# A two-layer graph network on one core: chunks 3 and 0 turned into features in halves, one more place for tiles, and a fixed list of eight steps in the second sweep

## Chip, core and metric

The kernel runs on one core of a Trainium2 chip. The metric is the time of one execution on the device in microseconds. The kernel before took 341.48 us (median of three runs, 340.38 to 344.35).

## What is computed

`x` has 4096 nodes with 64 features each. `adj` is a 4096 x 4096 float32 matrix in which about one entry in 128 is not zero. Two layers follow each other, each with a residual:

```python
h = relu(layernorm(x))                       # layer 0: two hops, x1 and x2
for k in range(2):
    h = tanh(concat([adj @ h, h]) @ W[k])
x = x + h
h = relu(layernorm(x))                       # layer 1: weighted neighbours
support = h @ weight
mask = adj != 0
rank = cumsum(mask, axis=1); deg = rank[:, -1:]
k = minimum(deg, 100); pos = rank - (deg - k)
w = mask * where(pos > 0, 0.5 ** (k - pos), 0)
x = x + w @ support + bias
```

Layer 0 needs the values of `adj` twice, once for each hop, and the second hop of a row needs the first hop of all rows. Layer 1 needs only where `adj` is not zero, and how many such entries follow in the same row: the weight of an entry is a power of two with that number as exponent.

## The kernel before

The 4096 nodes are four chunks of 1024 (CW), each of eight blocks of 128 (CB). A tile is a piece of `adj`, transposed by the host: 128 source nodes of one block by the 1024 destination nodes of one chunk, 512 KB. "Chunk" stands for destinations (I) or sources (J or g), "block" (b) for 128 sources.

**Sweep 1** reads all of `adj`, 1 MB (two blocks) at a time, row of chunks by row of chunks (0, 1, 2, 3). TensorE forms the first hop of each row from the weighted features (`acc_low`, L302), and for sources whose x1 is known already a part of the second hop (`acc`, same line). VectorE and ScalarE turn each tile into a byte code per entry (L267 to L283), which stays in SBUF: `code[g][J]` is 8 KB per partition for a pair of chunks. `settle` (L471) brings the codes of a row into their last form, once the row's counts are known. The tiles pass through a ring of five places of two blocks each, and through code places that are not filled yet.

`hxs[q]` holds for chunk q, per block, 64 columns of x1 (or h) and behind them 64 columns of the weighted features (`at(b)[:, :D]` and `at(b)[:, D:]`). There are four such tiles; `hx0` is reused when sweep 1 is over.

**Sweep 2** (`sweep2`, from L931) finishes layer 0 and does layer 1. Its work for TensorE is of three kinds:

- Hops (`hop`, L302 by `agg_pair`, and L987): 72 blocks of `adj` are read again, in the order `plan`: two or more blocks of chunk 2, eight of chunk 3, the rest of chunk 2, 24 of chunk 1, 24 of chunk 0. A block is two matmuls of 64 columns x 512, which the profile records as four; it needs its tile from HBM (L949, L951).
- The way from a chunk's sum to its layer-1 features (`finish_x2`), a chain across engines: copy the sum (L685 or L688), multiply (`py`, L697), add (L703), tanh (L707), residual (L712), layer norm (L196 to L202, with a power on GpSimd, L202, and the bias on GpSimd, L718), scale and maximum (L205), split into a high and a low part (`feat`, L743, L744). [...]
- Units of layer 1 (`layer1`, L870): 128 units, one for each source chunk J, destination chunk g and tile n. A unit is two matmuls of 128 columns x 512. It needs the features of chunk J and its weights, which are made from the codes by ScalarE in one instruction (an exponential, L810) or by VectorE in two (L802 makes the bits of a power of two, L805 scales it). Weights need a place of 4 KB per partition (`spaces`): ring pairs that are no longer loaded, code pairs whose units are done, the `after` rows, `hx1`, `hx2`; `hx0` holds the bits of VectorE's conversion.

The sums of a destination chunk over several J stay in PSUM where `kept` has the pair (four pairs). Else they are evicted to `parts` and added there (`evict`, L895 to L901). `finish_out` (L918, L925) multiplies by the layer's weight, adds, and writes out.

What sets the order: every engine runs its own instructions in the order in which the program emits them, and the program is written by a planner. `clock` holds the planner's estimate for each engine (a block 0.86, a unit 0.465, a conversion 0.96 on ScalarE and 1.4 on VectorE), `use` advances it, and tiles have an estimated landing. Before, the loop at the end of `sweep2` goes on with hops as long as tiles have landed by the estimate, and with units where they are runnable, but leaves 56 units (`n_late`) for after the last hop. `decode` decides which engine converts the next weights; `run_chain` resumes `finish_x2` when its clock is reached. SP issues all loads in the same order, each after the place it writes has been read.

Of the kernel before, what the change touches and what calls it, by code (L numbers as in the profile page):

```python
# [19 lines left out]
P = 128  # L20
# [24 lines left out]
def gnn_kernel(  # L45
# [50 lines left out]
    hxs = [place([P, CB, 2 * D], F32, f"hx{q}", "hx") for q in range(NCH)]  # L96
    at = lambda b: hxs[b // CB][:, b % CB, :]
# [129 lines left out]
    def weighted(I):  # L227

        v = by_t(flat(pre1[:, chunk(I), :]))
        pt = (one if I % 2 else two)(name="pg")  # L230
        for t in range(TC):
            nc.tensor.matmul(  # L232
                pt[:, t * P : (t + 1) * P].rearrange("p (c e) -> p c e", c=NC),
                v[:, t // 2, t % 2, :], wz[:, :, 0, 0, :],
                start=True, stop=True, skip_group_check=True,
            )
        nc.scalar.copy(
            as_nodes(hxs[I][:, :, D:]), pt.rearrange("p (t c e) -> p t c e", t=TC, c=NC)
        )
# [79 lines left out]
    def features_T(I):  # L319

        pt = (two if I % 2 else one)(name="ph")
        for t in range(TC):
            for c in range(NC):
                nc.tensor.matmul(
                    pt[c * D : (c + 1) * D, t * P : (t + 1) * P],
                    hxs[I][:, c * TC + t, :D], ident, start=True, stop=True, skip_group_check=True,
# [53 lines left out]
    def finish_first(acc, quads):  # L380
# [4 lines left out]
        def x1_half(c):  # L385
# [14 lines left out]
            for h in range(2):  # L400
                nc.scalar.copy(
                    as_nodes(hxs[0][:, :, :D])[:, 2 * h : 2 * h + 2, c], nodes(banks[h])[:, :, 0, c]
                )

        def hop1(b):
            for c in range(NC):
                nc.tensor.matmul(  # L407
                    G[c * D : (c + 1) * D, :], at(b)[:, :D], part_of(quads[c, b // 4], b),
# [33 lines left out]
    def finish_row(I, acc):  # L442
# [9 lines left out]
        take(hxs[I][:, :, :D], banks, 0)  # L452
# [26 lines left out]
    def sweep1():  # L479
        b0 = NB - CB // 2  # L480
        load_x(NCH - 1)
        first = ln_relu(hxs[-1][:, CB // 2 :, :D], pre1[:, b0:, :])
# [53 lines left out]
        for k in range(2 * NQ):  # L536
# [15 lines left out]
            if k == 0:  # L552
                rest = ln_relu(hxs[-1][:, : CB // 2, :D], pre1[:, NB - CB : b0, :])
                for g in (2, 1, 0):
                    lns[g] = ln_relu(hxs[g][:, :, :D], pre1[:, chunk(g), :])
                ends = []
                for n in (CB // 2, 0):
                    v = slice(n, n + CB // 2)
                    ends.append(ln_relu(hxs[2][:, v, :D], pre1[:, 2 * CB :, :][:, v]))
# [6 lines left out]
            for b in (4 * q + n for n in (2, 3, 0, 1)):  # L566
                h = b % 2
                nc.tensor.matmul(  # L568
                    low0[c][h * D : (h + 1) * D, :], at(b)[:, :D], part_of(a, b),
# [28 lines left out]
        for k in range(2 * NQ, len(units)):  # L598
# [16 lines left out]
            for r in (1, 0):  # L615
                g = b - 1 + r
                last = n == HB - 1 and r == 0
                agg_pair(acc[1], at(g)[:, D:], a[:, r], g == NB - 1, last)
                if fused(I, g):
                    agg_pair(  # L620
                        acc[0][:, 0, :], at(g)[:, :D], a[:, r], g == (3 if I == 1 else CB * I - 1), last
# [26 lines left out]
    def finish_last(acc):  # L648
# [10 lines left out]
        take(hxs[I][:, :, :D], banks, 0)  # L659
# [19 lines left out]
    def finish_x2(I, acc):  # L679


        h = chunk(I)
        S = tmp(name="S")
        if clock["ACT"] <= clock["DVE"]:
            nc.scalar.copy(S, acc)  # L685
            t = use("ACT", 0.6, clock["PE"] + 0.2) + 0.1
        else:
            nc.vector.tensor_copy(S, acc)  # L688
            t = use("DVE", 0.7, clock["PE"] + 0.2) + 0.1
        xres = residual(I)  # L690
        state["gap"] = 1.35, 2.2
        yield t

        pt = one(name="py")
        v = by_t(S)
        for t in range(TC):
# [5 lines left out]
        y = tmp([P, CB, D], name="y")  # L702
        nc.vector.tensor_tensor(  # L703
            as_nodes(y), pt.rearrange("p (t c e) -> p t c e", t=TC, c=NC), as_nodes(pre1[:, h, :]),
            op=ALU.add,
        )
        nc.scalar.activation(y, y, AF.Tanh)  # L707
        t = use("DVE", 0.7, use("PE", 1.15, t) + 0.2)
        state["gap"] = 0.6, 2.7
        t = use("ACT", 0.65, t + 0.1)  # L710
        yield t - 0.5
        nc.vector.tensor_add(pre1[:, h, :], xres, y)  # L712
        state["fetch"] = True
        t = use("DVE", 0.7, t + 0.1)
        ln = ln_relu(None, pre1[:, h, :])
        next(ln)
        t = use("DVE", 1.4, t)
        nc.gpsimd.tensor_tensor(  # L718
            pre1[:, h, :], pre1[:, h, :],
            bias_b[:, None, :].to_broadcast([P, CB, D]), op=ALU.add,  # L720
        )
        state["gap"] = 0.0, 1e9
        t = use("ACT", 0.65, t + 0.1) + 0.1
        yield t
        next(ln)
        t = use("POOL", 2.6, use("DVE", 0.9, t) + 0.1) + 0.1
        yield t
        try:
            next(ln)
        except StopIteration as stop:  # L730
            h2 = stop.value
        t = use("DVE", 0.7, t)
        while (
            state["done"] < CB * NCH * (2 - I)
            or I == 2 and any(w is lent[2] for w, _ in made[state["done"] :])
        ):
            yield clock["PE"] + 0.3
        if I == NCH - 1:
            feats[I] = feats[1] = place([P, CB, 2 * D], F32R, "mbuf", "feat")
        elif I == 0:  # L740
            feats[I] = feats[2]
        hi, lo = feats[I][:, :, :D], feats[I][:, :, D:]
        nc.vector.tensor_scalar(hi, h2, SCALE, None, op0=ALU.mult)  # L743
        nc.vector.scalar_tensor_tensor(  # L744
            lo, h2, SCALE, hi.bitcast(F32), op0=ALU.mult, op1=ALU.subtract
        )
        ready[I] = use("DVE", 1.2, t + 0.1) + 0.2


# [29 lines left out]
    order = {3: (0, 1, 2, 3), 2: (3, 0, 1, 2), 1: (2, 3, 0, 1), 0: (0, 1, 2, 3)}  # L779
    kept = {(3, 3), (2, 2), (1, 0), (1, 1)}  # L780
    units = [(J, g, n) for J in range(NCH - 1, -1, -1) for g in order[J] for n in range(CB)]
# [6 lines left out]
    state = {"wide": True, "fetch": True, "done": 0, "lead": 5.0, "dve": False, "dlead": 2.0, "gap": (0.0, 0.0)}  # L788

    def convert(engine=None):  # L790
        i = len(made)
        J, g, n = units[i]
        spaces.sort(key=lambda v: v[1])
        w, t = spaces.pop(0)
        v = (J, g, n % 2)
        if v in settled:
            settle(settled.index(v))
            done[J, g] = use("DVE", 1.25)
        t = max(t, done.get((J, g), 0.0) + 0.1)
        q = code[g][J][:, n, :]  # L800
        if engine == "DVE" or not engine and state["dve"] and max(clock["ACT"], t) + 0.96 > max(clock["DVE"], t) + 1.4:
            nc.vector.tensor_scalar(  # L802
                state["bits"], q, float(ZERO), ONE, op0=ALU.subtract, op1=ALU.mult
            )
            nc.vector.tensor_scalar(  # L805
                w, state["bits"].bitcast(F32), 2.0 ** (127 - LOW), None, op0=ALU.mult
            )
            t = use("DVE", 1.4, t)
        else:
            nc.scalar.activation(w, q, AF.Exp, scale=LN2, bias=BIAS)  # L810
            t = use("ACT", 0.96, t)
        made.append([w, t + 0.1])

    def decode():
        while True:
# [5 lines left out]
            if ahead <= 2 and state["done"] < len(units) and units[state["done"]][0] in ready:  # L821
# [7 lines left out]
            t = min((v[1] for v in spaces), default=1e9)  # L829
            if n == len(units):  # L830
                t = 1e9
            act, dve = (max(clock[e], t) for e in ("ACT", "DVE"))
            late = clock["DVE"] <= clock["PE"] + state["dlead"]
# [4 lines left out]
            elif (  # L838
                state["dve"] and late and dve + 1.4 <= d_end and dve <= clock["PE"] + 3.0
                and dve + 1.4 < act + 0.96 + (0.0 if len(spaces) < 3 else 1.0)  # L840
            ):
                convert("DVE")
# [261 lines left out]
```

## Time and profile before

| | |
|---|---|
| median of the runs shown | 341.48 us (340.38 to 344.35) |
| the profiled execution itself | 343.04 us |
| its span in the profile | 341.3 us |
| granted TensorE clock | 1.00 |
| TensorE busy | 329.6 us, 1578 matmul records |
| VectorE busy | 280.4 us |
| ScalarE busy | 190.5 us |
| read from HBM | 107.15 MB |

By stretches of the span (us from its start; busy time of each engine; what the DMA moved):

| stretch | what it is | length | PE | VectorE | ScalarE | GB/s |
|---|---|---|---|---|---|---|
| 26.6 to 191.9 | sweep 1 after its start | 165.3 | 165.3 | 153.7 | 75.6 | 304 to 421 |
| 194.4 to 207.5 | first hops of sweep 2 | 13.1 | 13.0 | 9.2 | 4.0 | 365 |
| 207.5 to 223.8 | hops up to the first unit | 16.3 | 14.6 | 9.5 | 3.0 | 408 |
| 223.8 to 255.7 | hops of chunk 1, first units | 31.9 | 31.9 | 22.2 | 18.1 | 405 |
| 255.7 to 303.0 | hops of chunk 0, units | 47.3 | 47.3 | 39.6 | 44.9 | 213 |
| 303.0 to 315.4 | units while chunk 0 becomes features | 12.4 | 10.9 | 11.3 | 10.4 | 0 |
| 315.4 to 341.3 | last units and outputs | 25.9 | 22.3 | 14.4 | 16.6 | 41 |

In the profile PE is TensorE's matmul, PEld its weight load, DVE is VectorE, ACT ScalarE, POOL GpSimd and SP the engine that issues the DMAs. "L302" is line 302 of the kernel. A name such as `accl` is a tile of the program. The profile says of an idle stretch which instruction's end released the waiting one. Matmuls are pipelined and their ends are modelled, so that TensorE can look busy while it runs below its pace. One execution is profiled; its instruction durations are used below.

### The profile page before, as it was taken

To read this page: it belongs to the slowest core of one execution; us is meant where nothing else is said; L and a number is where in the kernel's file an instruction comes from. 1 tells how busy PE (TensorE), PEld (TensorE's weight loads), DVE (VectorE), ACT (ScalarE), POOL (GpSimd) and SP (SyncE) were. 2 spreads that over 40 slices of the span, in tenths; PEclk is the share of its full clock that TensorE was granted. 3 is DMA by queue.
4 is the path that set the end of the run, shared out by engine and by line. 5 is a ranking of instruction groups with operands and counts; after the bars stand their busy time and mean duration, and the time that the engine had idled before them with its cause. 6 is when DMAs were issued, how large, how long until landed. Compare 5 with 4: busy or idle time off the path is not lost.

```text
span 341.3 us, 4305 instructions
## 1 busy us (share of the span) xinstructions
PE 329.6 (97%) x1578; PEld 150.1 (44%) x1578; DVE 280.4 (82%) x439; ACT 190.5 (56%) x199; POOL 23.5 (7%) x21
## 2 busy tenths in 40 slices
PE   8699999999999999999999999899999999998995
PEld 2354433433334333343333433143454656466885
DVE  4869999999999999999969683779456799889933
ACT  2493673285444590233480424037468999969990
POOL 2340000000000000000000000312003000003000
PEclk9999999999999999999999999999999999999999
DMA  7999999999999889976999999999996946500012
GB/s 265 420 423 420 424 415 427 418 422 421 421 418 423 371 321 419 356 270 219 381 361 292 324 356 411 409 409 407 407 396 237 344 151 219 198 17 0 2 52 71
DMA packets 22404, 108.47 MB, mean 318 GB/s; under 512 B 2416, under 2 KB 3824, under 8 KB 14320
## 3 DMA queue, kind: packets, MB, share of 16 engines
q1 hardware_dynamic: 22384, 108.21, 81.3%
q8 instruction: 12, 0.20, 0.2%
q14 instruction: 8, 0.07, 0.1%
HBM read 107.15 MB, written 1.05 MB: 317 GB/s over the span
## 4 chain that ended last, share of the span: by engine, by line
PE 82%; DMA 12%; DVE 3%; ACT 1%; SPq 0%; issue 0%
PE acc_low L302 25%; PE acc L302 20%; PE accl L870 16%; PE acc L987 6%; DMA codes<-in_adjA_dram 5%; DMA ring<-in_adjA_dram 5%; PE acc L568 4%; PE pto L918 2%; PE acc L407 2%; DMA wb<-in_weights_dram 2%; PE pt L370 2%; PE py L697 1%; PE acc_low L568 1%; PE po L215 1%; PE pg L232 1%; PE pt L396 1%
## 5 line engine op out<-in xcount | busy, mean ns | idle before, releaser
L810 ACT ACTIVATE weights<-codes 128x1024 fp32r<-128x1024 uint8 x91 | 87.6, 1044 | 7.0 <-PE accl L870 4.4
L302 PE MATMUL acc<-ring,hx 128*64 128x512 f32 x352 | 86.3, 597 | 1.7 <-DMA ring<-in_adjA_dram 1.7
L302 PE MATMUL acc_low<-ring,hx 128*64 128x512 f32 x264 | 65.5, 593 | 0.0
L870 PE MATMUL accl<-weights,feat 128*128 128x512 f32 x254 | 62.9, 399 | 1.5 <-DVE feat L744 1.5
L870 PEld LDWEIGHTS accl<-weights,feat 128*128 128x128 f32 x254 | 46.2, 188 | 20.7 <-ACT weights L810 7.1
L302 PEld LDWEIGHTS acc<-ring,hx 128*64 128x64 f32 x352 | 23.6, 136 | 52.5 <-issue 39.8
L471 DVE TENSOR_TENSOR codes<-codes,after 128x2048 uint16<-128x2048 uint16 x32 | 38.2, 1218 | 0.1
L302 PEld LDWEIGHTS acc_low<-ring,hx 128*64 128x64 f32 x264 | 19.0, 137 | 37.5 <-issue 37.4
L267 ACT ACTIVATE codes<-ring 128x2048 int8<-128x2048 f32 x10 | 19.1, 1908 | 27.7 <-DMA ring<-in_adjA_dram 27.6
L283 DVE TENSOR_SCALAR mbuf<-ring 128x2048 uint8<-128x2048 f32 x28 | 34.2, 1221 | 0.0
L268 ACT ACTIVATE codes<-codes 128x2048 uint8<-128x2048 int8 x17 | 32.5, 1910 | 0.5
L276 DVE TENSOR_SCALAR cnt<-codes 128x1024 uint16<-128x1024 uint16 (+1 forms) x80 | 29.9, 373 | 2.7
L275 DVE TENSOR_TENSOR codes<-mbuf,cnt 128x1024 uint16<-128x1024 uint16 (+1 forms) x51 | 30.0, 588 | 1.9
L805 DVE TENSOR_SCALAR weights<-bits 128x1024 fp32r<-128x1024 f32 x36 | 25.9, 719 | 6.1 <-PE accl L870 2.2
L302 PE MATMUL acc_low<-codes,hx 128*64 128x512 f32 x120 | 27.8, 593 | 0.0
L802 DVE TENSOR_SCALAR bits<-codes 128x1024 uint32<-128x1024 uint8 x36 | 24.9, 691 | 0.8
L718 POOL TENSOR_TENSOR pre<-pre,wb 128x512 f32<-128x512 f32 x4 | 5.4, 1360 | 270.3 <-DVE xc L197 260.6
L987 PE MATMUL acc<-ring,hx 128*64 128x512 f32 x96 | 21.9, 598 | 0.0
L283 DVE TENSOR_SCALAR mbuf<-codes 128x2048 uint8<-128x2048 f32 x17 | 20.7, 1220 | 0.0
L202 POOL TENSOR_TENSOR s<-s,half 128x8 f32<-128x8 f32 (+1 forms) x10 | 16.9, 1688 | 18.2 <-DVE s L201 18.2
L275 DVE TENSOR_TENSOR codes<-codes,cnt 128x1024 uint16<-128x1024 uint16 (+1 forms) x24 | 13.9, 580 | 3.7 <-ACT codes L268 2.4
L302 PEld LDWEIGHTS acc_low<-codes,hx 128*64 128x64 f32 x120 | 8.5, 137 | 17.0 <-issue 17.0
(98 smaller groups left out, 275.4 us busy)
## 6 DMA issues: line engine op xcount, KB each, us to landing
ring<-in_adjA_dram SPq DMA_DIRECT2D x74, 512.0 KB, 7.9
ring<-in_adjA_dram SPq DMA_DIRECT2D x37, 1024.0 KB, 8.2
codes<-in_adjA_dram SPq DMA_DIRECT2D x26, 1024.0 KB, 17.7
pre<-in_x_dram SPq DMA_DIRECT2D x4, 256.0 KB, 6.9
xres<-in_x_dram SPq DMA_DIRECT2D x4, 256.0 KB, 8.7
out_dram<-o SPq DMA_DIRECT2D x3, 256.0 KB, 2.5
out_dram<-o SPq DMA_DIRECT2D x2, 128.0 KB, 2.2
wb<-in_weights_dram SPq DMA_DIRECT2D x1, 192.0 KB, 6.3
```

Source lines behind the costliest of these rows:

```text
L267: nc.scalar.activation(sign, tile_of(I, a), AF.Sign)
L268: nc.scalar.activation(m, sign, AF.Square, scale=float((FLAG - 1 + 0.25) ** 0.5))
L275: nc.vector.tensor_tensor(q, m, cnt, op=ALU.add)
L276: nc.vector.tensor_scalar(cnt, q, 0x7F7F, None, op0=ALU.bitwise_and)
L283: nc.vector.tensor_scalar(m, tile_of(I, a), 0.0, float(FLAG - 1), op0=ALU.not_equal, op1=ALU.mult)
L302: nc.tensor.matmul(acc[c * D : (c + 1) * D, :], src, a[:, c * C : (c + 1) * C], start=first, stop=last,)
L471: nc.vector.tensor_tensor(q, q, a[:, None, :].to_broadcast([P, 4, CW // 2]), op=ALU.subtract)
L802: nc.vector.tensor_scalar(state["bits"], q, float(ZERO), ONE, op0=ALU.subtract, op1=ALU.mult)
L805: nc.vector.tensor_scalar(w, state["bits"].bitcast(F32), 2.0 ** (127 - LOW), None, op0=ALU.mult)
L810: nc.scalar.activation(w, q, AF.Exp, scale=LN2, bias=BIAS)
L870: nc.tensor.matmul(sums[g][:, c, :], feats[J][:, k, :], w[:, c * C : (c + 1) * C], start=first, stop=last,)
L987: nc.tensor.matmul(accs[0][c * D : (c + 1) * D, :], at(b + h)[:, :D], tiles[n + c][2][:, h * C : (h + 1) * C], start=(0, b + h) == firsts[ ...
```

## The change

The diff changes four things in sweep 2, and one in how the features lie.

1. The x1 features (`hxs`) and the weighted features (`gxs`) get tiles of their own, two chunks in each: `hx0`, `hx1`, `gx0`, `gx1`. `gx1` becomes a place for tiles of sweep 2, loaded as its first tile, and from tile 50 on a place for weights; `gx0` takes the part that `hx0` had, then holds bits of VectorE's conversion, then weights. Three ring pairs (KEEP) are reloaded to the end instead of four; code pairs whose units are done (`tile_pairs`) become places for tiles too.
2. `finish_x2` does chunks 3 and 0 (`SPLIT`) in two halves of 256 columns, with instructions of half the size alternating between engines. The order of a chunk's units is changed so that the first half's four come first. `ready` is kept for each half. Chunk 3's hop comes after two blocks of chunk 2, not four.
3. Sums of a pair of destination chunks (`in_low`) go to the banks of `plow` as a third set; nine pairs are kept in PSUM instead of four. Orders of destinations change with it.
4. A list of eight steps, `steps2`, says how many hops and how many units are to be done in turn: 22 hops, 9 units, 29 hops, 14 units, and so on to 72 hops and 128 units. The search for what is runnable and `n_late` go.
5. VectorE may convert two units at once (two L802, then two L805), with two tiles for the bits.

```diff
-    hxs = [place([P, CB, 2 * D], F32, f"hx{q}", "hx") for q in range(NCH)]
-    at = lambda b: hxs[b // CB][:, b % CB, :]
+    hxs, gxs = (
+        [v[:, q] for r in range(NCH // 2) for v in [place([P, 2, CB, D], F32, f"{n}{r}", n)] for q in range(2)]
+        for n in ("hx", "gx")
+    )
+    at, weighted_at = (lambda b, v=v: v[b // CB][:, b % CB, :] for v in (hxs, gxs))
...
     def finish_x2(I, acc):
+        split = I in SPLIT
+        parts = [slice(0, 1), slice(1, 2)] if split else [slice(0, 2)]
+        tiles = [slice(2 * u.start, 2 * u.stop) for u in parts]
...
+        for a in tiles:
+            b = slice(2 * a.start, 2 * a.stop)
+            nc.vector.tensor_tensor(nodes_(y[:, b]), sums_[:, a], x2[:, a], op=ALU.add)
+            nc.scalar.activation(y[:, b], y[:, b], AF.Tanh)
...
+        for a in tiles:
+            b = slice(2 * a.start, 2 * a.stop)
+            nc.vector.tensor_tensor(nodes_(y[:, b]), xres[:, a], nodes_(y[:, b]), op=ALU.add)
+            nc.vector.tensor_reduce(s1[:, b], y[:, b], axis=AX.X, op=ALU.add)
+            nc.vector.scalar_tensor_tensor(
+                xc[:, b], wide(s1[:, b]), -1.0 / D, y[:, b], op0=ALU.mult, op1=ALU.add
+            )
+            nc.scalar.activation(sq[:, b], xc[:, b], AF.Square)
...
+            nc.gpsimd.tensor_tensor(s2[:, b], s2[:, b], half[:, b], op=ALU.pow)
...
+            nc.vector.tensor_scalar(hi, xc[:, b], SCALE, None, op0=ALU.mult)
+            nc.vector.scalar_tensor_tensor(
+                lo, xc[:, b], SCALE, hi.bitcast(F32), op0=ALU.mult, op1=ALU.subtract
+            )
+            for u in range(a.start // 2, a.stop // 2):
+                ready[I, u] = t
...
-    order = {3: (0, 1, 2, 3), 2: (3, 0, 1, 2), 1: (2, 3, 0, 1), 0: (0, 1, 2, 3)}
-    kept = {(3, 3), (2, 2), (1, 0), (1, 1)}
-    units = [(J, g, n) for J in range(NCH - 1, -1, -1) for g in order[J] for n in range(CB)]
+    order = {3: (0, 1, 2, 3), 2: (1, 2, 3, 0), 1: (2, 3, 0, 1), 0: (1, 0, 2, 3)}
+    spilled = {(3, 0), (2, 1), (1, 2)}
+    kept = {(J, g) for J in range(1, NCH) for g in range(NCH)} - spilled
+    in_low = {(3, 2), (1, 1), (0, 2)}
+    units = [
+        (J, g, n) for J in range(NCH - 1, -1, -1) for g in order[J] for n in (0, 1, 4, 5, 2, 3, 6, 7)
+    ]
+    SPLIT = {0, 3}
...
-        KEEP = 4
+        KEEP = 3
+        GX = 50
+        steps2 = [(22, 9), (29, 14), (34, 19), (39, 22), (46, 33), (50, 41), (56, 61), (72, 128)]
-        plan = [(2, 16, 20), (3, 24, 32), (2, 20, 32), (1, 16, 32), (1, 8, 16), (0, 8, 32)]
+        plan = [(2, 16, 18), (3, 24, 32), (2, 18, 32), (1, 16, 32), (1, 8, 16), (0, 8, 32)]
...
+            elif k == 1 and n < GX:
+                load(k, r, a, t)
+            elif k == 1:
+                space(place([P, CW], F32R, "gx1", "weights"), t)
...
+        load(1, 0, place([P, CW], F32, "gx1", "ring"), -20.0)
         for n, k in enumerate(rings):
...
-            cap = len(units) - (n_late if n < total else 0)
-            units_ = runnable(cap, 0.1)
...
+            while steps2 and n >= steps2[0][0] and state["done"] >= steps2[0][1]:
+                steps2.pop(0)
+            to = steps2[0] if steps2 else (total, len(units))
...
+            elif n < to[0] and n + (not blocks[n][0]) < len(tiles):
+                n += hop(n)
+            elif i < to[1] and half_of(units[i]) in ready and (len(made) > i or spaces):
+                layer1()
+            elif chain:
+                clock["PE"] = max(clock["PE"], chain[0][0])
```

## The prediction

> **What bounds the kernel now.** I read the page's busy shares first, then the busy time of the engines in stretches, then the chain of work that ended last, and last the order of time on TensorE and ScalarE where the chain leaves TensorE.
>
> ```profile
> PE 329.6 (97%) x1578; PEld 150.1 (44%) x1578; DVE 280.4 (82%) x439; ACT 190.5 (56%) x199; POOL 23.5 (7%) x21
> ...
> PEclk9999999999999999999999999999999999999999
> ```
>
> TensorE is busy for 97% at its full granted clock, so no edit off TensorE can win more than its gaps. A busy share hides part of these, because a matmul's end is modelled. So I look at what the chain says of sweep 2, which begins at 191.9 us (columns: start, us, what):
>
> ```profile
> 191.87 0.58 ACT x1T L221
> ...
> 197.81 8.58 DMA ring<-in_adjA_dram
> 206.43 1.08 PE acc L302 x4
> ...
> 211.41 9.04 DMA ring<-in_adjA_dram
> 220.59 1.08 PE acc L302 x4
> ...
> 228.98 1.13 PE accl L870 x4
> 230.11 2.73 PE acc L302 x12
> ...
> 313.41 0.61 DVE xc L205
> 314.05 0.44 DVE feat L743
> 314.51 0.70 DVE feat L744
> 315.35 7.54 PE accl L870 x32
> ...
> 330.25 3.72 PE accl L870 x16
> ```
>
> Read here: two transfers on the chain (tiles late), then TensorE alternating between hops (L302: four records, one block) and layer-1 units (L870: two records, one unit), then VectorE's features of chunk 0 (L744). Prices: a unit 3.72/8 = 0.465 us; a block 0.858 (2.73 less the 0.16 for turning back, below, over 3); turning to units 1.13 - 2 x 0.465 = 0.20; turning back 0.15 (3.58 for four blocks).
>
> How late the tiles are, from TensorE's order of time (start, us, then the idle time before in brackets):
>
> ```profile
> 211.56 1.08 PE L302 MATMUL acc<-ring,hx 128*64 128x512 f32 x4 [0.18 <-DMA ring<-in_adjA_dram]
> 212.83 1.08 PE L302 MATMUL acc<-ring,hx 128*64 128x512 f32 x4 [0.20 <-DMA ring<-in_adjA_dram]
> 214.11 1.08 PE L302 MATMUL acc<-ring,hx 128*64 128x512 f32 x4 [0.20 <-DMA ring<-in_adjA_dram]
> ```
>
> Blocks start 1.275 us apart where TensorE needs 0.858: this stretch goes at the DMA's pace.
>
> TensorE's sum from 191.85 (end of sweep 1's matmuls) to 337.75 (end of the last output product) is 145.9 us. Work: 70 blocks x 0.858 = 60.1; 128 units x 0.465 = 59.5; four `py` 4.1; `pt` and counts 2.5; `pto` 7.4; together 133.6. The other 12.3 us: A, 2.3 for `x1T` before `pt` (191.85 to 196.69 less 2.5 of work); B, 4.2 for tiles (196.69 to 223.74 is 27.05, with 24 blocks and two `py` = 22.9 in it); C, turns, 12 x 0.20 + 11 x 0.15 = 4.05; D, 1.5 for chunk 0's features. A, B, C and D give 12.1. What the change can win lies in B, C and D.
>
> The engines that make weights for the units are nearly full too:
>
> ```profile
> 274.05 26.63 ACT L810 ACTIVATE weights<-codes 128x1024 fp32r<-128x1024 uint8 x28
> ```
>
> That is 0.951 us per conversion with no gap; VectorE takes about 1.55 us for its two instructions (L802, L805: starts 1.52 to 1.56 apart). Together 0.59 us a unit against 0.465 on TensorE, so a long run of units lives on stock.
>
> **What the Trainium skill says.** ScalarE: Activation LUTs, What ACT_TABLE_LOAD costs: an ACTIVATE with immediates takes 186 ns + 0.833 ns per element and successive ones overlap by about 93 ns. For 1024 elements that is 1039 and 946; the trace has 1044 and 951. VectorE: DVE Perf Modes, The TRN2 errata: an fp32 two-input operation takes (N+151)/0.96 ns: 691 for 512, 424 for 256; the trace has 690 and 424. So a half costs 61% of a whole, and halves cost VectorE work. Perfetto Trace Analysis, Identifying Dependency Chains: the same gap repeating can mean that there isn't enough SBUF for the next tile. The trace agrees for the end of sweep 1: from 176 to 190 us the DMA moves 308 GB/s, and ring pairs of 1.05 MB come free each 3.43 us (four products of 0.858), which is 306 GB/s; from 200 to 206 us it moves 415.
>
> **The change, part by part.**
>
> *The extra place (split hx).* After it, the weighted features have tiles of their own, and `gx1` (chunks 2 and 3) has its last reader about 165 us, in the middle of row 3. SP issues its load right behind sweep 1's last load (175.1 us); before, SP then waited 3.0 us for PE. The DMA has room there (308 of 415), so the tile displaces none, and behind `xres` one more tile goes out in the hole of 196 to 200 us (282 GB/s). From then on the DMA is full in both, so tile n lands when tile n-1 landed before: tile 17 (counted from 0) at 210.3, 18 at 211.55, then each 1.275. Sum: 10 blocks from 196.69 end at 205.27, the first `py` at 206.41; blocks 12 to 17 follow without waiting to 211.56; 18 ends at 212.4; 19, 20, 21 wait for 212.8, 214.1, 215.4; block 21 ends at 216.2. Waits: 1.2 us.
>
> *Chunk 3 first and in halves.* Its hop ends two blocks earlier (1.7 us) and `py` ends at 206.4 instead of 208.6. Before, from `py`'s end to L744's end took 10.2 us (208.58 to 218.76). In halves, the first half's path: y, tanh (0.42), both halves' add, reduce, xc (6 x 0.45), s2 (0.43 + 0.17), pow on 128x4 (1.01 against 2.14 for 128x8), then xc, hi, lo (0.45 + 0.30 + 0.45): 6.9 us with the hand-overs, ready at 213.3; the second half 214.5. The list calls for the nine units at 216.2, so neither is waited for. VectorE and ScalarE pay about 1.3 and 0.4 us more per split chunk; chunk 3's is hidden by the settling steps (L471), which are moved behind it and needed later.
>
> *The nine units.* Weights have five places by then (the lent one and two ring pairs, which are not reloaded). Unit 5 on wait for ScalarE, which converts into a place only once it is read: 217.1 + 4 x 0.951 puts unit 8 at 221.0, so the run ends at 221.5 instead of 220.6: 0.8 us lost.
>
> *The fixed list.* TensorE turns to units 8 times and back 7, 2.65 us against 4.05: 1.4 won. It also leaves 67 units instead of 56 behind the last hop, 35 of them not of chunk 0, two ahead of `py`. Before, 22 stood between `py` and chunk 0's units (10.2 us) and the wait was 1.5; now 33 (15.3 us) cover the chain's path: D goes, 1.5 won. What is late next is the conversion. 67 units take TensorE 31.2 us plus `py` and two `pto`, 35.7 in all, from 293.1 to 328.8. By the order of the program 21 are in stock then, ScalarE makes 33 and VectorE 13. ScalarE: 33 x 0.951 + halves of S, tanh, square (2.1) ends near 327, 1.5 before the last unit; at each unit between I find 1.1 us or more in hand. VectorE: its chain and the evictions of J = 1 end at 305, then pairs (two L802, two L805 without waiting on each other). The trace shows no such pair: 1.20 us a unit if independent starts are 0.60 apart (as in the L901 copies), 1.55 if nothing is won; I take 1.25. The cover is gone if ScalarE starts its 29 in a row over 1.1 us late.
>
> *Kept sums.* 14 eviction steps instead of 24 (10 adds of 0.68 fewer on VectorE), and the last group is copied by two engines. No matmul is added; the copies hide beside units, as 24 did.
>
> *DMA later on.* Seven places rotate instead of eight, joined by freed code pairs. Between blocks 22 and 46 TensorE needs 1.4 us per tile (24 blocks and 22 units), the DMA 1.275, and the queue (8.7 us from issue to landing) turns seven places in about 9.6 us, 1.37: I put it at nothing, at most 1 us.
>
> **Sum.** B 4.2 to 1.2: -3.0; nine units +0.8; C -1.4; D -1.5: -5.1 us. Span 341.3 to 336.2; that execution's 343.04 would be 337.9. It stood 1.6 above the median of the runs, 341.48; so 336.4.
>
> **The rivals.** *No tile earlier*: the DMA was full, not short of places (for it: its share is 0.94 from 176 to 190 us; against: 306 and 308 GB/s agree). Block 21 then starts at 216.6: +1.3, 337.7. *The tail starves*: VectorE's pairs win nothing or its chain is late, and ScalarE's last run starts late; each unit short costs 0.5 to 0.6, I take five: +3.0, 339.4. For it: at 315.3 us the weight load already waited 1.9 for L810. *Slower, ScalarE alone feeds the groups*: the list doesn't turn back to hops when weights are missing, so if VectorE's conversions stand behind its chains and settling, the groups of 9, 11, 8 and 20 run beyond their stock (5, 6, 6, 8) at 0.951: 23 x 0.486 = 11.2, 0.8 of it counted: +10.4, 346.8. It turns slower than before from eleven such units on (5.1/0.486). Against: at 250 us ScalarE has some seven us in hand.
>
> **Numbers.** Forecast 0.58; no tile earlier 0.14; starved tail 0.16; slower 0.08; better, the waits of 1.2 and 0.8 gone too, 334.4: 0.04. Range 334.4 to 339.4. About 1% is what a measurement tells from no change: under 338.1 is faster, 0.70; within 0.21; slower 0.09.
>
> **What would show it.** Right: the last hop ends near 293, TensorE's waits on L744's successor vanish, the first unit follows block 21 near 216, and the last `pto` ends near 332.7. Wrong: waits of the unit matmuls on ScalarE or VectorE weights of more than 2 us, or hops waiting for tiles after 222 us.

## The result and the profile after

The changed kernel takes 339.12 us (median of 14 runs, 337.12 to 342.82). The kernel before took 343.25 us in the 14 runs beside it. The ratio is 0.9889, with a 95% interval of 0.9856 to 0.9922: 3.8 us faster (2.7 to 4.9). The forecast was 336.4, so the direction is right and the time 2.7 us too low. Two steps made most of that, and this section and the runs below separate them: the last one of the sum, from the profiled execution to the median of the three runs shown (some 1.5 us), and "DMA later on", put at nothing. With smaller terms that partly cancel, the sum of the gains is some 1.2 us off.

The profiled execution of the changed kernel took 338.05 us, its span is 336.3 us. Lines in the new kernel have moved: the first hops are L305 (before L302), the hops of chunk 0 L1081, units L934 (L870), ScalarE's weights L849 (L810), VectorE's L854 and L859, features L779 and L780 (L743, L744), `pto` L992. Busy shares and clock on the page:

```profile
PE 326.8 (97%) x1578; PEld 151.3 (45%) x1578; DVE 274.8 (82%) x446; ACT 191.8 (57%) x204; POOL 23.0 (7%) x23
...
PEclk9799999999999999999999999999999999999999
```

TensorE's share is the same 97%, which shows how little this number says. The clock dips in the second slice; traces of both kernels have such a dip, and it is taken up at the end. The chain of work that ended last (start, us, what):

```profile
197.30 8.73 PE acc L305 x40
206.03 1.14 PE py L708 x8
207.17 8.82 PE acc L305 x40
215.99 2.51 PE accl L934 x10
...
218.67 0.93 ACT weights L849
219.61 1.05 ACT weights L849
...
241.20 8.76 DMA ring<-in_adjA_dram
250.00 1.08 PE acc L305 x4
...
295.59 22.25 PE accl L934 x98
317.83 1.82 PE pto L992 x16
```

Of the two transfers of before none is left ahead of the units: 20 blocks and `py` run from 197.3 to 216.0 without a gap. Two conversions of ScalarE stand on the chain in the group of nine units. One transfer is new, at 250 us. The way through chunk 0's features is gone: 49 units follow the last `py` in one run. On this trace the forecast's sum looks right to 0.1 us: span 336.3 against 336.2, last `pto` at 332.7 as forecast.

That agreement is partly luck, as further traces of both kernels show. Sweep 2 is taken here from the first `pt` matmul to the end of the last `pto` (the prediction's 145.9 us begins about 2 us earlier). "Tiles" is TensorE's idle time before matmuls that waited for a tile in sweep 2:

| trace | first `pt` at | sweep 2 | tiles |
|---|---|---|---|
| before | 193.75 | 143.98 | 1.7 |
| before, second (f1_before) | 195.41 | 142.83 | 1.3 |
| before, third (g3_before) | 195.83 | 144.10 | 1.8 |
| changed | 194.30 | 138.44 | 0.2 |
| changed, second (e1_again) | 195.17 | 138.73 | 0.2 |
| changed, third (g4_after) | 192.66 | 140.87 | 1.6 |
| changed, fourth (h2_again) | 192.54 | 140.51 | 1.4 |

The means are 143.64 and 139.64: 4.0 us, close to the 3.8 of the timed runs. The first pair alone says 5.5.

### The profile page after: what moved, and what is told of

It is laid out like the page before. It is cut to its first block, busy times and chain, and to the rows that moved or that the text cites. A ratio compares the mean times of both kernels' runs of the same rounds, so it can differ in the third digit from the quotient of the medians.

```text
span 336.3 us, 4329 instructions
## 1 busy us (share of the span) xinstructions
PE 326.8 (97%) x1578; PEld 151.3 (45%) x1578; DVE 274.8 (82%) x446; ACT 191.8 (57%) x204; POOL 23.0 (7%) x23
## 4 chain that ended last, share of the span: by engine, by line
PE 92%; DMA 5%; ACT 1%; SPq 1%; issue 0%; DVE 0%; ACTq 0%
PE acc_low L305 25%; PE acc L305 22%; PE accl L934 17%; PE acc L1081 6%; DMA ring<-in_adjA_dram 5%; PE acc_low L571 4%; PE acc L571 4%; PE pto L992 2%; PE acc L410 2%; PE pt L373 2%; PE py L708 1%; PE pg L235 1%; PE po L218 1%; PE ph L327 1%; PE pt L399 1%; ACT weights L849 1%
## 5 line engine op out<-in xcount | busy, mean ns | idle before, releaser
L849 ACT ACTIVATE weights<-codes 128x1024 fp32r<-128x1024 uint8 x92 | 88.7, 1043 | 11.3 <-PE accl L934 7.3
L305 PE MATMUL acc<-ring,hx 128*64 128x512 f32 x352 | 84.4, 595 | 0.2 <-DMA ring<-in_adjA_dram 0.2
L305 PE MATMUL acc_low<-ring,gx 128*64 128x512 f32 x264 | 65.5, 593 | 0.0
L934 PE MATMUL accl<-weights,feat 128*128 128x512 f32 x250 | 61.2, 397 | 0.4 <-ACT weights L849 0.4
L934 PEld LDWEIGHTS accl<-weights,feat 128*128 128x128 f32 x250 | 45.8, 188 | 16.5 <-ACT weights L849 5.9
L305 PEld LDWEIGHTS acc<-ring,hx 128*64 128x64 f32 x352 | 24.3, 137 | 49.0 <-issue 45.3
L305 PEld LDWEIGHTS acc_low<-ring,gx 128*64 128x64 f32 x264 | 19.0, 137 | 37.5 <-issue 37.4
L859 DVE TENSOR_SCALAR weights<-bits 128x1024 fp32r<-128x1024 f32 x33 | 22.1, 691 | 16.5 <-PE accl L934 8.5
L305 PE MATMUL acc_low<-codes,gx 128*64 128x512 f32 x120 | 27.8, 593 | 0.0
L757 POOL TENSOR_TENSOR s<-s,half 128x4 f32<-128x4 f32 (+1 forms) x6 | 8.2, 1370 | 222.8 <-DVE s L753 222.8
L854 DVE TENSOR_SCALAR bits<-codes 128x1024 uint32<-128x1024 uint8 x34 | 22.7, 687 | 0.1
L1081 PE MATMUL acc<-ring,hx 128*64 128x512 f32 x96 | 21.2, 594 | 0.0
L224 ACT COPY x1T<-acc 64x512 f32<-64x512 f32 x6 | 3.5, 579 | 25.5 <-PE acc L305 25.5
L305 PEld LDWEIGHTS acc_low<-codes,gx 128*64 128x64 f32 x120 | 8.5, 137 | 17.0 <-issue 17.0
```

What stands on the lines that cost most here:

```text
L305: nc.tensor.matmul(acc[c * D : (c + 1) * D, :], src, a[:, c * C : (c + 1) * C], start=first, stop=last,)
L854: nc.vector.tensor_scalar(bits[k - n], q, float(ZERO), ONE, op0=ALU.subtract, op1=ALU.mult)
L859: nc.vector.tensor_scalar(w, bits[k - n].bitcast(F32), 2.0 ** (127 - LOW), None, op0=ALU.mult)
L934: nc.tensor.matmul(sums[g][c], feats[J][:, k % TC * NC + k // TC, :], w[:, c * C : (c + 1) * C], start=first, stop=last,)
L1081: nc.tensor.matmul(accs[0][c * D : (c + 1) * D, :], at(b + h), tiles[n + c][2][:, h * C : (h + 1) * C], start=(0, b + h) == firsts[0], sto ...
```

## The experiments

Times are medians; the kernel before took 342.93, 342.9, 342.66 and 342.18 in the four sets (34, 48, 29 and 14 runs). The changed kernel took 339.12, 338.94 and 339.34 where it was timed.

**The changed kernel again (e1_again), unchanged.**

> The changed kernel once more, nothing edited. Theory (the sum of the prediction holds for every execution and only the step from one execution to the median was off): sweep 2, from the end of sweep 1's matmuls to the end of the last output product, takes 140.3 us within 0.5 as in its first profile, and the ratio to the kernel before is 0.985. Rival (the changed kernel has executions in which sweep 2 itself is slower, by late tiles or weights): sweep 2 of this execution lies anywhere from 140 to 144 us, and the ratio stays near 0.989.

338.94 us, ratio 0.9885 (0.9849 to 0.9922): the ratio is the one that the rival named, while the trace repeats the short sweep 2 of the theory. This execution took 339.22 us, with a first `pt` matmul 0.9 us later than in the first trace. The third and the fourth trace (below) decide for the rival.

**Without the extra place (e2_noplace).**

```diff
-        load(1, 0, place([P, CW], F32, "gx1", "ring"), -20.0)
```

> The changed kernel without the load into gx1: one tile less is on its way at the start of sweep 2, and six places rotate instead of seven. The list of steps is as in the changed kernel. Theory of the prediction (the extra place brings every tile 1.28 us forward at the start and is worth nothing later): blocks 12 to 21 wait about 1.3 us more than in the changed kernel, time +1.3 us. Rival (the number of places in rotation is what counts, since SP stands still while units run): also holes in the DMA after 222 us, waits of the hops for tiles there, time +3 us or more.

342.53 us, ratio 1.0001 (0.9970 to 1.0032): in this kernel all the rest together wins nothing. TensorE's order of time in this kernel (start, us, then the idle time before):

```profile
213.65 1.08 PE L305 MATMUL acc<-ring,hx 128*64 128x512 f32 x4 [0.19 <-DMA ring<-in_adjA_dram]
215.94 1.08 PE L305 MATMUL acc<-ring,hx 128*64 128x512 f32 x4 [1.22 <-DMA ring<-in_adjA_dram]
...
252.39 1.08 PE L305 MATMUL acc<-ring,hx 128*64 128x512 f32 x4 [0.21 <-DMA ring<-in_adjA_dram]
...
321.26 2.10 PE L992 MATMUL pto<-wb,parts 128*128 128x64 f32 x16 [0.69 <-DVE parts L965]
```

Its sweep 2 is 143.47 us, 3.8 above the mean of the changed kernel. Up to the eleven units after block 45 it loses 2.5 (they start 60.42 us after the first `pt`, against 57.93 in the mean of the four traces), by tiles. That is twice what the theory on record had (1.3), and the rival's sign is there: from 222 to 230 us the DMA moves 164 GB/s, against 241 in the changed kernel, and hops wait for tiles at 235, 237, 251 and 252 us. The other 1.3 are a by-product in the tail: the planner puts another pair of conversions ahead of an eviction, and `pto` waits for it.

**No chunk in halves (e3_whole).**

```diff
-    SPLIT = {0, 3}
+    SPLIT = set()
```

> The changed kernel with no chunk split in halves (all four as chunks 2 and 1). Theory of the prediction: chunk 3's features are ready 10.2 us after its first product ends, at about 217.3 us instead of 213.7 (first half), and the list calls for them at 216.0: TensorE waits 1.3 us; chunk 0's 12.5 us are covered by 33 units (15.3 us), nothing lost: time +1.3 us. Rival (the split is covered on both ends and is worth nothing): +0.0 to 0.3 us. Other rival (the split costs more on VectorE than it wins): faster by 0.5 us.

341.43 us, ratio 0.9944 (0.9920 to 0.9968): some 2.3 us slower than the changed kernel, where the theory said 1.3. The first unit waits for chunk 3's features:

```profile
215.92 0.73 PE L934 MATMUL accl<-feat 128*128 128x512 f32 x2 [1.59 <-DVE feat L780]
```

Chunk 0, whole as well, causes no wait in this trace, and the stretch from the units after block 45 to the end takes 81.81 us, against 81.70 to 81.73 in four traces of the changed kernel. So what the halves gain here, they gain at chunk 3. How much of the 1.59 us is left at block 45 is not settled by traces: the units there start 59.97 us after the first `pt` in this run and 57.83 in g2_whole56, which has the same list up to block 50 and the same wait.

**67 late units in the kernel before (e4_late67).**

```diff
-        n_late = 56
+        n_late = 67
```

> The kernel before with one number edited: 67 units instead of 56 left for after the last hop, the rest as before. Theory of the prediction (chunk 0's features were late by 1.5 us and more units in front of them hide that): the wait for L744 goes, time -1.5 us against the kernel before. Rival (the weights of 67 units can't be made in time without the pairs on VectorE and the fewer evictions): waits for L810 or L805 in the tail, time between -0.5 and +2 us.

345.31 us, ratio 1.0083 (1.0049 to 1.0117): slower by 2.4, more than the rival had (2). The wait for chunk 0's features (1.5 us before) is gone, and weights are late in its place:

```profile
320.87 0.73 PE L870 MATMUL accl<-weights,feat 128*128 128x512 f32 x2 [0.23 <-ACT weights L810]
321.81 0.73 PE L870 MATMUL accl<-weights,feat 128*128 128x512 f32 x2 [0.21 <-ACT weights L810]
```

The idle times are small, but these units start 0.94 us apart, which is ScalarE's conversion and not TensorE's 0.465; the 49 units after `py` take 24.7 us instead of 22.8. Tiles are late too: ten blocks of chunk 0 in one run take 10.1 us, against 9.0 to 9.4 in the kernel before. In the kernel before, then, 67 late units alone win nothing.

**The kernel before, second and third trace (f1_before, g3_before), unchanged.**

> The kernel before once more, unchanged, for a second trace. Theory 'sweep 1 scatters': the time from the first pt matmul to the end of the last pto matmul repeats within 0.3 us (143.98 in the first trace of before), and what differs is the time of the first pt matmul (192.6 to 195.9 us in the six traces so far, of which five share sweep 1's order). Rival 'sweep 2 scatters': sweep 2 comes out at 142.5 or less, because its tiles land at other times from run to run, and the forecast's comparison of two single executions overstates the gain.

> The kernel before for a third trace: sweep 2 of 142.8 to 144.0 us as in the two so far, with waits for tiles of 1.3 to 1.7 us in all. Theory 'what scatters is the start of sweep 1 and, by up to 1.2 us, the tiles of sweep 2': the first pt matmul between 192.5 and 196 us. Rival 'the first trace was an unusually long sweep 2': 142.8 or below again, and the forecast's sum was made against an execution whose sweep 2 was 1 us longer than usual.

In the table above. Both ideas hold in part: the start scatters by 2 us, and sweep 2 by 1.3, so that the trace which the forecast used had a sweep 2 that was 0.3 above the mean.

**The place is given to weights after one tile (f2_gx0).**

```diff
-        GX = 50
+        GX = 0
```

> The extra place gx1 takes the one tile at the start of sweep 2, and becomes a place for weights as soon as that tile is used, where the changed kernel refills it with tiles up to the fiftieth. Theory 'a lead of one tile is kept only by a place in rotation': tiles 12 to 21 wait as in the run without the place (some 2.4 us), and the time is 341.5 to 342.5 us beside a median of 339.0 for the changed kernel. Rival 'the head start of one tile is what counts, the transfers are then limited by their rate': the waits stay at 0.2 to 0.4 us and the time is 339.0, or less, since the units have a place more. A time of 340.5 to 341.5 would say that the 1.4 us which the run without the place lost in its tail came from the missing place for weights, not from tiles.

341.09 us, ratio 0.9954 (0.9929 to 0.9979). The tiles of blocks 18 to 21 start 1.27 us apart again, tile waits are 1.6 us in all, and the units after block 45 start 59.14 us after the first `pt`. By the time, the reading on record for 340.5 to 341.5 would be that the tail's loss came from the missing place for weights. The trace contradicts it: weights have the place here, and yet `pto` waits 0.82 us for the same eviction, and the tail takes 83.0 us, as in the run without the place (81.7 in the changed kernel). What differs between the two runs lies ahead of the tail: by the traces this one loses 1.2 us there and the other 2.5, and the medians are ordered the same way. So a lead of one tile is lost in part when its place is not refilled; the head start alone keeps some of it, and the rest needs the place in rotation. How they share is not shown, since 59.14 lies within the scatter of the changed kernel.

**Three more pairs of turns (f3_turns).**

```diff
-(50, 41), (56, 61), (72, 128)]
+(50, 41), (52, 46), (54, 51), (56, 56), (58, 61), (72, 128)]
```

> The changed kernel with three more turns between hops and units: the 20 units between blocks 50 and 58 come in four groups of five instead of 20 at block 56. The forecast priced a pair of turns at 0.35 us (0.20 into the units and 0.15 out of them), so sweep 2 is 1.05 us longer and the time 340.0 beside 339.0. Rival 'a turn is hidden or costs only where something is late': no change, within 0.3 us. If weights or tiles wait in addition, more than 1.5.

339.89 us, ratio 0.9913 (0.9879 to 0.9948), which is too wide to tell 1 us by the medians. In the trace it can be told: from the eleven units after block 45 to the end are 82.87 us, against 81.70 to 81.73 in the four traces of the changed kernel. That is 1.15 for three pairs, 0.38 each; the forecast priced 0.35.

**Seven units first instead of nine (f4_seven).**

```diff
-steps2 = [(22, 9), (29, 14), (34, 19), (39, 22), (46, 33)
+steps2 = [(22, 7), (29, 14), (34, 19), (39, 24), (46, 33)
```

> The changed kernel with seven units instead of nine after block 22, and five instead of three after block 39. The two waits for weights in the first group (0.21 us each, with restarts some 0.9 in all) are gone. Theory 'weights limit that group': 0.9 us less, 338.1 beside 339.0. Rival 'the transfers set the time up to block 45': the wait for a tile near 250 us grows by what was saved, or tiles wait in blocks 29 to 39 as well, and the time is 339.0 or above.

340.34 us, ratio 0.9922 (0.9895 to 0.9950): no gain, and neither theory's reason. The first group waits for nothing now, and the second waits more:

```profile
229.39 0.73 PE L934 MATMUL accl<-weights,feat 128*128 128x512 f32 x2 [1.41 <-ACT weights L849]
...
238.28 0.73 PE L934 MATMUL accl<-weights,feat 128*128 128x512 f32 x2 [0.73 <-ACT weights L849]
```

ScalarE made no weights between 221.0 and 228.3 us in this kernel: chunk 2's copy, tanh and square stand there. A unit moved between groups takes its conversion along, into another neighbourhood on ScalarE. The DMA's pause moves too, and this matters for the account below: SP, which issues the loads, waits 4.1 us for the first hop after the first group, and 6.2 us for the one after the second, which now takes 5.65 us. From 222 to 230 us the DMA moves 344 GB/s instead of 241, and then (length, busy time of PE, PEld, DVE, ACT, POOL, then clock, DMA share, GB/s):

```profile
230.00:236.00 6.00, 5.78 (x25) 2.13 (x25) 5.09 (x8) 3.12 (x4) 1.82 (x1) 1.00 0.59 185
```

**56 late units, with halves (g1_late56) and without (g2_whole56).**

```diff
-(50, 41), (56, 61), (72, 128)]
+(50, 41), (56, 72), (72, 128)]
```

The second kernel has `SPLIT = set()` too.

> The changed kernel with 31 units instead of 20 after block 56, so that 56 late units are left as before the change, 22 of them between chunk 0's last sum and its own units. Theory of the forecast: either part alone ends the wait for chunk 0's features. The halves are ready 8.3 and 10.5 us after the sum's last matmul, the units in between take 22 x 0.47 = 10.3 us, and half 1 is first needed four units later: no wait, sweep 2 as in the changed kernel (138.4 to 138.8 us), 339.0. Rival 'the split is not enough': a wait of 1 us or more at chunk 0's first unit. Second rival: 31 units in one group run out of weights, 0.5 to 1.5 us of waits for weights ahead of 285 us.

> As the run with 56 late units, and no chunk in halves. Theory: now chunk 0's features come too late again, ready 12.5 us after the sum's last matmul and needed after 10.3: a wait of some 2 us at chunk 0's first unit, on top of the 1.6 us for chunk 3's features that the run without halves showed: sweep 2 of 143.5 to 144 us, 343 us. Rival 'the new order of units and the conversions in pairs alone shorten the features' step': no wait at chunk 0, sweep 2 of 141.8, 341.4 as with 67 late units.

341.21 us (0.9959; 0.9926 to 0.9992) and 343.88 us (1.0026; 1.0003 to 1.0049). Neither trace shows a wait for chunk 0's features, against the theory for the second. The features are there 10.05 us after the last `py` matmul without halves (before: 11.5 us; the 12.5 in the expectation counts from the first one), just under the 22 units' 10.2, so nothing is to spare. What costs time in both traces is the group of 31 units, in the first kernel thus:

```profile
279.07 1.67 PE L934 MATMUL accl<-weights,feat 128*128 128x512 f32 x6 [0.22 <-ACT weights L849]
280.96 1.68 PE L934 MATMUL accl<-weights,feat 128*128 128x512 f32 x6 [0.22 <-ACT weights L849]
```

Four such waits stand in that group. They make only 0.87 us of idle time, but the group takes 16.55 us where 31 units and a turn would be 14.6. Sweep 2 is 141.30 us with halves, 142.31 without. The second figure must be read with care: its trace is of the fastest of 19 runs, 340.19 us, and the median of 343.88 is near what the theory gave (343). Where the ordinary execution of this kernel loses the other 3.7 us is not shown.

**The changed kernel, third and fourth trace (g4_after, h2_again), unchanged.**

> The changed kernel for a third trace: sweep 2 of 138.4 to 138.8 us as in the two so far. Theory 'sweep 2 of the changed kernel scatters by its tiles too' (the run with more turns, which is the same up to block 50, reached the units after block 45 at 57.8 us after the first pt matmul, against 56.7 and 57.0): 138.4 to 139.6 us, and the two traces so far were at the short end, which is why the medians differ by 1 us less than the traces. Rival: 138.4 to 138.8 again, and the missing microsecond lies in sweep 1.

> The changed kernel once more, timed beside the run with two units moved. Theory 'its sweep 2 scatters by its tiles': 138.4 to 140.9 us in the trace, by the waits for tiles between 236 and 252 us; median 338.8 to 339.3.

338.84 us for the one, a median of 339.34 (0.9904; 0.9866 to 0.9943) for the other. Both sweeps 2 are 2 us longer than in the first two traces. In the third trace, order of time on TensorE:

```profile
240.34 1.08 PE L305 MATMUL acc<-ring,hx 128*64 128x512 f32 x4 [0.57 <-DMA ring<-in_adjA_dram]
241.85 1.08 PE L305 MATMUL acc<-ring,hx 128*64 128x512 f32 x4 [0.44 <-DMA ring<-in_adjA_dram]
...
250.81 1.08 PE L305 MATMUL acc<-ring,hx 128*64 128x512 f32 x4 [0.20 <-DMA ring<-in_adjA_dram]
```

The first two are blocks 37 and 38, the last is block 45, where the forecast let the tiles be in time. The last of the waits, at block 45, ends at 250.00, 251.19, 250.81 and 250.35 us in the four traces, while the first `pt` matmuls are spread over 2.6 us: an execution that starts early loses its lead here.

**Two units moved ahead of the late tiles (h1_fill, h3_fill_look).**

```diff
-(39, 22), (46, 33), (50, 41)
+(39, 24), (46, 35), (50, 41)
```

> The changed kernel with two more units after block 39 (five instead of three) and two fewer after block 50, so that more other work lies between the blocks whose tiles were late. Theory 'tiles 34 to 46 come at the rate of the transfers after the hole at 222 to 230 us': the waits for tiles between 236 and 252 us, which were 0.2, 0.2, 0.7 and 1.6 us in the traces with the changed kernel's list, are at most 0.2 us, the units after block 45 are reached with the same work done but up to 1 us sooner on average, and the time is 338.2 beside 339.0 for the changed kernel. Rival 'nothing was lost there': the two units only move, 339.0. If their weights are late instead, as in the run with seven units, 340 or more.

> A second trace of the kernel with two units moved from block 50 to block 39: waits for tiles between 236 and 252 us of at most 0.2 us, sweep 2 of 138.2 to 138.7 us. Rival: waits that scatter up to 1.6 us as in the changed kernel.

338.11 us (six runs, 337.5 to 338.74; ratio 0.9874, 0.9839 to 0.9908) and 337.85 us for the single one. Waits for tiles are 0.2 and 0.4 us, sweep 2 is 138.27 and 138.71. It is the fastest kernel here, and it points to the theory; but its interval overlaps that of the changed kernel beside it, and no trace of it began as early as 192.6 us. So its lead of a microsecond is not shown.

## Why the forecast was right in direction and wrong in size

**The step from the trace to the median failed first.** "It stood 1.6 above the median of the runs, 341.48" took three runs for the kernel's median. With 14 to 48 runs the median is 342.2 to 343.3, and the profiled execution's 343.04 is an ordinary one. Without that subtraction the same sum gives 337.9. This step moves the time forecast and not the gain: of the 5.1 us that the sum promised, 3.8 were measured.

**"DMA later on: nothing, at most 1 us" failed second.** The step compared means: 1.4 us of TensorE per tile against 1.275 of DMA, a reserve of 3 us over 24 tiles. It left out that a group of nine units takes no tile for 5.5 us, so that the places are full and no further tile is issued. SP's waits show it (changed kernel, 196 to 260 us; in all, times, longest):

```profile
SPq L1034 <- PE acc L305: 27.2, 26, 6.1
```

The longest, 6.1 us, is for the first hop after the nine units; between 205 and 256 us of the kernel before no wait of SP for a hop is over 2.6. Stretches of the changed kernel (from:to, length, busy time of PE, PEld, DVE, ACT, POOL, then clock, DMA share, GB/s):

```profile
222.00:230.00 8.00, 8.00 (x41) 3.52 (x36) 4.62 (x7) 2.60 (x4) 0.73 (x1) 1.00 0.79 241
230.00:236.00 6.00, 6.00 (x28) 2.39 (x27) 4.87 (x6) 4.42 (x5) 3.13 (x2) 1.00 1.01 402
236.00:242.00 6.00, 6.00 (x28) 2.82 (x29) 5.72 (x8) 4.37 (x5) 0.00 (x0) 1.00 0.98 326
242.00:250.00 8.00, 7.81 (x36) 2.59 (x30) 2.16 (x4) 3.54 (x4) 0.00 (x0) 1.00 1.03 416
```

The same stretch of the kernel before, which had its units in groups of two to five:

```profile
222.00:230.00 8.00, 8.00 (x37) 3.59 (x36) 6.30 (x8) 2.53 (x4) 1.59 (x1) 1.00 1.03 410
```

(410 - 241) GB/s x 8 us are 1.35 MB, 2.6 tiles or 3.3 us of DMA: the whole reserve. Two more things set the depth of the hole: with six places instead of seven it is 164 GB/s (e2_noplace), and with a shorter first group and a longer second one it moves behind the second (f4_seven). The kernel before had eight places besides its small groups, and the runs don't share out the difference between the two. After the hole the tiles come just in time or late. In the first trace seven blocks and a turn take 6.62 us (244.39 to 251.01) instead of 6.16, a loss of 0.5. The units after block 45 start 56.71, 57.03, 59.16 and 58.82 us after the first `pt`, so the losses are 0.5, 0.8, 2.9 and 2.6, 1.7 in the mean. From 216 to 230 us the four traces move 4.2 to 4.4 MB, and the kernel before 5.7, so the hole is much the same in all four; the two that start early need the tiles behind it sooner, and lose most. "Hops waiting for tiles after 222 us" stood in the forecast as a sign of error. That the pause makes the hole is shown by SP's waits. That the hole makes the later tiles late fits the runs, but it was not taken away alone, and why an early start is given back was not tried.

**The extra place** did what was forecast, and a bit more. In the first trace waits in blocks 12 to 21 went from 4.2 to some 0.2 us, not to 1.2, and block 21 ends at 215.9 instead of 216.2, although sweep 1 ended 0.5 later. The rival "no tile earlier" is refuted: without the place, or without its refilling, the waits come back (e2_noplace, f2_gx0).

**The nine units** lost 1.07 us, not 0.8: 5.45 us (215.92 to 221.37) less nine units of 0.465 and a turn of 0.20. **Chunk 3's halves** were ready at 213.7 and 215.9, forecast 213.3 and 214.5; the second was there as the group began, about 2 us before its own unit. Its lateness is one instruction: the second half's `xc` took 1.52 us where the first half's took 0.43. GpSimd's power for it was done at 213.42, so it did not wait for that; GpSimd's bias, which the change puts behind the powers of a chunk in halves, ran at the same time:

```profile
212.48 0.43 DVE L764 SCALAR_TENSOR_TENSOR xc<-xc,s 128x256 f32<-128x256 f32 x1 [0.61 <-POOL s L757]
213.62 1.52 DVE L764 SCALAR_TENSOR_TENSOR xc<-xc,s 128x256 f32<-128x256 f32 x1
```

```profile
213.40 1.45 POOL L760 TENSOR_TENSOR pre<-y,wb 128x512 f32<-128x512 f32 x1
```

In all four traces of the changed kernel and for both chunks in halves this `xc` takes some 1.52 us and ends 0.3 us after the bias. That the bias holds it up was not tried by moving the bias.

**D, chunk 0's features,** went as forecast, for more reasons than needed. 33 units without halves (e3_whole), halves with 22 units (g1_late56), or neither of them (g2_whole56, in one trace and with nothing to spare) all end the wait. Where the chunk is whole, the features' step is 1.0 to 1.5 us shorter than before, and the runs don't separate why. The worth of 67 late units in the changed kernel is that the group of 31 is avoided.

**The turns** cost 0.38 a pair for 0.35. **The tail** kept pace as forecast: ScalarE's last run ends at 327.1, and VectorE's pairs take 1.20 us a unit where 1.25 was taken:

```profile
299.54 27.58 ACT L849 ACTIVATE weights<-codes 128x1024 fp32r<-128x1024 uint8 x29
```

The sum, then: 143.98 less 5.1 is 138.9. Add 1.7 for late tiles and 0.3 for the nine units, take off 0.8 for earlier tiles, and it is 140.1, where the mean of four traces is 139.64; the 0.5 between them is not accounted for. The kept sums and the conversions in pairs were not tested by themselves.

## What to carry to other kernels

A transfer stream with a small reserve must be checked stretch by stretch against the places it can fill: here the longest pause of its consumer, and not the mean need, made the hole. Work that fills a wait should stand where the wait is, in small groups, and each piece brings its own supply along. And one trace against three runs is not a base: look at how far the kernel before scatters before turning a span into a forecast.

## What was not expected of the hardware

The start of the kernel decides part of when sweep 2 begins. TensorE waits for the first features and tiles before 13 us. Before and changed, first traces:

```profile
6.87 2.04 PE L568 MATMUL acc_low<-ring,hx 128*64 128x512 f32 x8
11.49 1.94 PE L568 MATMUL acc_low<-ring,hx 128*64 128x512 f32 x8 [2.59 <-DMA ring<-in_adjA_dram]
```

```profile
6.95 1.94 PE L571 MATMUL acc_low<-ring,hx 128*64 128x512 f32 x8 [1.20 <-DVE hx L208]
11.17 3.63 PE L571 MATMUL acc_low<-ring,hx 128*64 128x512 f32 x8 [2.29 <-DMA ring<-in_adjA_dram]
```

The same eight matmuls take 3.63 us instead of 1.94, and from 12 to 14 us the granted clock is 0.50 in the changed kernel. In all 17 traces of this study the granted clock between 10 and 17 us falls (to 0.59 to 0.73 in the lower of the parts from 10 to 13 and from 13 to 17 us) where TensorE's idle times between 4 and 13 us, in two or three pieces, add up to 3.49 us or more (eight traces), and stays at 1.00 where they add up to 3.15 or less (nine). The first `pt` matmul is at 194.3 to 195.9 us in the former and at 192.5 to 193.8 in the latter, whichever kernel it is. The Trainium skill, TensorE: Matmul & The Clock Gate, What's actually happening, says that the array falls to half its clock after an idle window of about 3.4 us. The traces agree in the rate, and the total at which it falls is near; but no single wait in them is over 2.9 us. So a wait of 3.4 us in one piece is not needed. Whether the sum decides, or where the waits fall, was not tried: it is read from 17 traces.

The timed runs carry each execution's mean clock over its span, in which a drop near the end counts as well. Of the kernel before, 76 runs at 0.996 or below have a median of 343.3 us and 49 runs above it 341.7. For the changed kernel the medians are 339.2 (16 runs) and 338.6 (14), so an undisturbed start is worth less there, as its traces say.
